# A graph-attention kernel on one core: chunks of blocks of 5, 8, 12 and 12 tiles in place of 8, 11, 11 and 7, rows in one ring, and a plan with more half steps

## The chip, the core and the metric

The kernel runs on one core of one Trainium2 chip. The metric is the device time in microseconds (us) of one execution. Before the change the median of three runs is 6028.87 us (6024.4 to 6030.63).

The engines are TensorE (PE in the profile; PEld is its weight load), VectorE (DVE), ScalarE (ACT), GpSimd (POOL) and the queue of SyncE (SP), which here only issues transfers. Each works through its own instructions in the order in which the program lists them.

## The reference

A layer of graph attention over 12,500 nodes and 412,500 edges (each of 200,000 in both directions, and a loop at every node), sorted by `dst`. Features are 128 wide, edge features 64.

```python
h = relu(layernorm(x))
h0, q, k, v = h @ Wn + bn, h @ Wq + bq, h @ Wk + bk, h @ Wv + bv
eh = edge_attr_64 @ We + be
attn_in = concatenate([q[src], k[dst], eh], axis=-1)
hmid = leaky_relu(attn_in @ A1 + b1, 0.2)
scores = leaky_relu(hmid @ A2 + b2, 0.2)
w = softmax(scores.mean(axis=-1), axis=0)            # over all edges
out = segment_sum(w[:, None] * v[dst], src, num_segments=12500)
y = h0 + out
x + gamma * (y - mean(y)) / sqrt(var(y) + 1e-5) + beta
```

## The kernel before, in words

**Edges come sorted by `dst` and are needed by `src`.** So the kernel sorts them on the way, in two stages that meet in tables in HBM. A *group* is 1024 edges (8 tiles of 128); there are 403 groups. A *block* is the 128 source nodes whose number leaves the same rest by 98; there are 98 blocks. A table has, for every block, room for a fixed number of tiles of 128 *slots*; a slot takes one edge's row of 257 numbers: its place in the block, the 128 of its hidden vector (without the q part) and the 128 of v.

The groups are cut into four *chunks* by `CHUNKS` (L55, L127 to L136), each with a table of its own. Before the change they hold 86, 121, 121 and 75 groups, and their blocks have 8, 11, 11 and 7 tiles.

- **Getting a chunk ready** (`ready`, L532): counts how many edges each block gets, and gives every edge its slot (`place_slots`, L455). This goes on by *slot steps* of 5 tiles of edges: two matmuls on PE into one bank (L478), a reduction on DVE (L522), a comparison on DVE (L471), a small scaling (L526). 646 of them in all: 138, 194, 194 and 120 for the four chunks. `clear_ends` (L163) writes zeros over the last two tiles of every block of a table.
- **First stage** (`first_stage`, L655): for each group, loads edge features, a window of k and v, and the offsets; in four *half steps* it makes rows with PE (L705, L708), moves them out of PSUM with ACT (L691), and lets POOL scatter each tile of 128 rows into its slots by an indirect DMA (L645, eight for a group).
- **Second stage** (`second_stage`, L718): for each block of a chunk, loads its slots (`load`, L725), adds the q part by a selection of nodes, takes the leaky ReLU, the scores, the exponentials against a running maximum, and sums the weighted v rows by node into `acc`. It works on *quads* of up to 4 tiles: two quads for blocks of 7 and 8 tiles, three for 11 and 12.

**What runs beside what.** L1012 to L1027 make five stretches. In the first, chunk 0 goes through its first stage while chunk 1 is made ready. In the next ones the second stage of a chunk runs beside the first stage of the chunk after it and beside the making ready of the one after that. In the last one only the second stage of chunk 3 is left. `interleave` (L63) puts the steps of these jobs in turn, by their shares. Before all this come the nodes' own matmuls, and after it a final normalisation.

**The plan of the second stage** (L871 to L905). A block i begins at step `2 * i0`; a quad takes two steps, so that blocks of two quads come every 4 steps and blocks of three every 6. `at(when, turn_, job, ...)` puts a job into a step and into one of four places in it (turn 0 to 3); jobs of the same place go by the number of the block, older first. Several blocks are under way at a time, each at another link of this chain: `turn` (PE: transposes and adds q), `steep` (ACT scales by 0.2, then DVE takes the larger of the two), `heads_of` (PE), `add_bias` (ACT), `leaky` (DVE), `by_slot` (PE), `scores` (DVE), `turn_top` (PE), `top_of_all` (DVE), `spread_top` (PE), `exponentials` (DVE, then ACT), `add_weights` and `weights` (DVE), `products` (PE), `add_sums` (DVE). All of it is in this order on the engines' queues: an engine that waits for one job holds back all that is listed behind it. Before it come `load`, then `places` (PE turns the places of the rows), `put_places` (ACT, and a DMA to HBM), `spread_places` (a DMA that spreads them over all partitions) and `select` (DVE).

Rows are held in a pool of six buffers of 11 tiles (`BUFS`, L37). A load is planned 17 steps ahead of its block (11 for two quads), and not before the `products` of the block six earlier (`load_at`, L907); `places` is planned 7 steps ahead. `LAG` (L35) is the number of steps from a block's start to its first `products`.

Of the kernel before, what the change touches and what calls it, by code (L numbers as in the profile page):

```python
# [10 lines left out]
FP = mybir.dt.float32  # L11
BF = mybir.dt.bfloat16
# [3 lines left out]
AF = mybir.ActivationFunctionType  # L16
ALU = mybir.AluOpType
AX = mybir.AxisListType
# [4 lines left out]
P = 128  # L23
D = 128
DE = 64
H = 8
EPS = 1e-5
SLOPE = 0.2
# [3 lines left out]
WIN = 42  # L32

QUAD = 4
LAG = 11  # L35

BUFS = 6  # L37

RROWS = 16

SPARE = 2

OTHER = 960

STR = 5

# [2 lines left out]
ROW = 2 * D + 1  # L49
# [2 lines left out]
MAGIC = float(3 << 22)  # L52

NGRP = 5
CHUNKS = (0.213, 0.3, 0.3, 0.187)  # L55
BECAUSE = "worked out within these bounds on the chip"


def _ceil(a, b):
    return -(-a // b)  # L60
# [44 lines left out]
def kernel(ctx: ExitStack, tc: tile.TileContext, n_edges, x, src, dst, ea, w_nv, w_qt, w_kt,  # L105
# [12 lines left out]
    nc = tc.nc  # L118
    NP = x.shape[0]
    NTN = NP // P  # L120
# [14 lines left out]
    NC = len(chunks)  # L135
    most_tiles = max(ct for _, _, ct, _ in chunks)  # L136

    blocks = []
    for c, (_, _, ct, _) in enumerate(chunks):
        for b in range(NTN):  # L140
            blocks.append((c, b, ct, _ceil(ct, QUAD), blocks[-1][4] + blocks[-1][3] if blocks else 0))
        assert 2 * QUAD >= ct > QUAD or 3 * QUAD >= ct > 2 * QUAD
# [6 lines left out]
    q_tab = dram.tile([NTN, P, 3 * D], BF, name="q_tab")  # L149
# [23 lines left out]
    ident = const.tile([P, P], FP, name="ident")  # L173
# [5 lines left out]
    ones = const.tile([P, P], FP, name="ones")  # L179
# [59 lines left out]
    t_bank = ps_t.tile([P, 512], FP, name="t_bank")  # L239
# [215 lines left out]
    def place_slots(c):  # L455
# [31 lines left out]
        def settle(t0, t1):  # L487
# [116 lines left out]
    most_of = late.tile([P, NTN], FP, name="most_of")  # L604
# [20 lines left out]

    main = ctx.enter_context(ExitStack())
    p1 = main.enter_context(tc.tile_pool(name="p1", bufs=2))
    pb = main.enter_context(tc.tile_pool(name="pb", bufs=BUFS))
# [4 lines left out]
    p3 = main.enter_context(tc.tile_pool(name="p3", bufs=1))  # L633
# [5 lines left out]
    def scatter(c, g, k, row, sent):  # L639
# [3 lines left out]
        if m > 0:  # L643
# [74 lines left out]
    def second_stage():  # L718


        rows_of, qws, plss, state = {}, {}, {}, {}
        state["s_ps"] = ps_s.tile([P, 512], FP, name="s_ps")
        nc.vector.memset(state["s_ps"], 0.0)

        def load(i):  # L725
            c, b, ct, _, _ = blocks[i]
            rows_of[i] = pb.tile([P, most_tiles, ROW], FP, name="rows_of")
            nc.sync.dma_start(out=rows_of[i][:, 0:ct, :],
                              in_=tabs[c][b * ct * P:(b + 1) * ct * P, :].rearrange("(p j) r -> p j r", p=P))
            qws[i] = ps.tile([P, 3 * D], BF, name="qw")  # L730
            nc.sync.dma_start(out=qws[i], in_=q_tab[b])

        def places(i):
            ct = blocks[i][2]
# [8 lines left out]

        def spread_places(i):
            ct = blocks[i][2]
            plss[i] = p1.tile([P, most_tiles * P], U8, name="pls")
            at = i % 4 * most_tiles
            nc.sync.dma_start(out=plss[i][:, 0:ct * P], in_=pl_d[at:at + ct, :].rearrange("t e -> (t e)").unsqueeze(0)
                              .to_broadcast([P, ct * P]))
# [8 lines left out]
        def turn(i, q):  # L758
# [7 lines left out]
            for k in range(3):  # L766
                nc.tensor.matmul(h_ps[:, 0:m * P], lhsT=qws[i][:, ts(k, D)], rhs=plss[i][:, q * QUAD * P:(q * QUAD + m) * P],  # L767
                                 start=False, stop=k == 2, skip_group_check=True)

        def steep(i, q):  # L770

            m = min(QUAD, blocks[i][2] - q * QUAD)
            h_ps = state.pop((i, q))[:, 0:m * P]
            low = p3.tile([P, QUAD * P], FP, name="low")[:, 0:m * P]
            nc.scalar.activation(low, h_ps, AF.Copy, scale=SLOPE)  # L775
# [39 lines left out]
            nc.vector.tensor_reduce(state["top"], score[:, 0:ct], AX.X, ALU.max)  # L815

        def turn_top(i):
            nc.tensor.transpose(state["s_ps"][0:1, P:2 * P], state["top"], ident)

        def top_of_all(i):  # L820
            state["top1"] = ps.tile([1, 1], FP, name="top1_of")
            nc.vector.tensor_reduce(state["top1"], state["s_ps"][0:1, P:2 * P], AX.X, ALU.max)

        def spread_top(i):
            nc.tensor.matmul(state["s_ps"][:, 2 * P:2 * P + 1], lhsT=ones[0:1, :], rhs=state["top1"], start=True, stop=True,
                             skip_group_check=True)

        def exponentials(i):
            _, b, ct, _, _ = blocks[i]
            before = (b - 1) % NTN  # L830
            nc.vector.tensor_max(most_of[:, b:b + 1], state["s_ps"][:, 2 * P:2 * P + 1], most_of[:, before:before + 1])

            shift = ps.tile([P, 1], FP, name="shift_of")
            nc.vector.tensor_scalar(shift, most_of[:, b:b + 1], -1.0 / H, None, op0=ALU.mult)
            score = state["score", i][:, 0:ct + 1]
            nc.scalar.activation(score, score, AF.Exp, bias=shift, scale=1.0 / H)

        def add_weights(i):
            _, b, ct, _, _ = blocks[i]
# [33 lines left out]
        def at(when, turn_, job, *args):  # L873
            plan_of.setdefault(when, []).append((turn_, len(plan_of[when]) if when in plan_of else 0, job, args))

        for i, (c, b, ct, nq, i0) in enumerate(blocks):
            t = 2 * i0
            at(load_at(i), 2, load, i)
            at(t - 7, 3, places, i)
            at(t - 6, 0, put_places, i)  # L880
            at(t - 5, 0, spread_places, i)
            at(t - 1, 3, select, i)
            for q in range(nq):
                at(t + 2 * q, 1, turn, i, q)
                at(t + 2 * q + 1, 0, steep, i, q)
            t += 2 * nq
            at(t - 1, 3, heads_of, i)
            at(t, 0, add_bias, i)
            at(t, 3, leaky, i)
            at(t + 1, 0, by_slot, i)  # L890
            at(t + 1, 3, scores, i)
            at(t + 2, 0, turn_top, i)
            at(t + 2, 3, top_of_all, i)
            at(t + 3, 0, spread_top, i)
            at(t + 3, 2, exponentials, i)
            at(t + 4, 3, add_weights, i)
# [10 lines left out]
    def load_at(i):  # L907

        _, _, _, nq, i0 = blocks[i]
        t = 2 * i0 - (17 if nq > 2 else 11)  # L910
        if i >= BUFS:
            _, _, _, nq, i0 = blocks[i - BUFS]
            t = max(t, 2 * (i0 + nq - 1) + LAG)
        return t

    def all_sums():

# [8 lines left out]
    def other_edges():  # L926

        with tc.tile_pool(name="others", bufs=1) as op, tc.tile_pool(name="others_ps", bufs=1, space=PSUM) as ops_:
# [5 lines left out]
            with tc.For_i(0, turns, 1) as g:  # L934
# [63 lines left out]
                with tc.For_i(0, NTN, 1) as b:  # L998
# [8 lines left out]
                    nc.vector.tensor_add(a, a, bank[:, 0:D])  # L1007

    second = second_stage()
    ends = [load_at(c * NTN) for c in range(NC)]  # L1010
    ends.append(2 * (blocks[-1][4] + blocks[-1][3]) + LAG)
    for c in range(NC + 1):  # L1012
        jobs = []
        if c < NC:
# [79 lines left out]
```

## Time and profile before

The profile is of one execution of its own: its span is 6619.4 us and its time 6621.16 us, against the median of 6028.87 us of the runs that are not profiled. Lengths in the text come from this execution.

| engine | busy us | share of the span |
|---|---|---|
| PE | 5232.6 | 79% |
| DVE | 4482.4 | 68% |
| POOL | 3374.8 | 51% |
| PEld | 3539.8 | 53% |
| ACT | 2122.2 | 32% |

Busy shares are means over stages that are limited by different things, so the stretches are looked at one by one. Their borders are seen in the first and last instructions of the lines that belong to one job: POOL's first scatter begins at 369.0 us and its last at 5702.8 us, the second stage's loads begin at 1393.7 us, and the last `add_sums` stands at 6476.0 us. A row of a table of stretches gives, for each engine, its busy time and the number of its instructions there, then the granted share of TensorE's clock (1.00 is full speed), the busy share of the 16 DMA engines, and GB/s.

### The profile page before, as it was taken

The numbers are of one execution on the slowest core, as the hardware profiler recorded it, in microseconds if no ns is written. First come the engines' busy times: TensorE is split into PE (matmuls) and PEld (weight loads), VectorE is DVE, ScalarE is ACT, GpSimd is POOL, SyncE is SP. The second block draws the span as 40 slices with busy tenths as digits, with TensorE's granted clock in tenths as the row PEclk, the third lists the DMA queues.
The fourth block names the chain that finished last, engine by engine and source line by source line (L and its number), as shares of the span: only waits on it lengthen the run. The fifth ranks groups of instructions, "written<-read, shape, count | busy, mean of one in ns | idle before, by whom it ended". The sixth has DMA issues, their size and how long they took to land. (4 is left out here: it accounts for less than half of the span.)

```text
span 6619.4 us, 99836 instructions
## 1 busy us (share of the span) xinstructions
PE 5232.6 (79%) x32180; PEld 3539.8 (53%) x32180; DVE 4482.4 (68%) x14096; ACT 2122.2 (32%) x5090; POOL 3374.8 (51%) x3236
## 2 busy tenths in 40 slices
PE   5665665568888888879888888888999999988881
PEld 3332433345555555556555555555766767655550
DVE  8755755556666666657666666665777777777778
ACT  3422122223333333333333333333433333333331
POOL 0057567765666666656666666665555555200000
PEclk8777677778898888989999999989999999999995
DMA  6755455566777777767778777776887878544443
GB/s 192 218 169 158 135 159 155 155 180 202 220 226 215 224 213 221 223 207 231 234 238 248 241 236 226 226 234 212 262 257 250 260 246 260 190 152 152 152 139 117
DMA packets 607563, 1362.14 MB, mean 206 GB/s; under 512 B 120100, under 2 KB 336860, under 8 KB 569016
## 3 DMA queue, kind: packets, MB, share of 16 engines
q1 hardware_dynamic: 423572, 880.87, 46.3%
q0 software_dynamic: 154704, 424.26, 17.7%
q10 hardware_dynamic: 28756, 50.57, 2.4%
q8 instruction: 255, 4.18, 0.3%
q14 instruction: 276, 2.26, 0.1%
HBM read 782.14 MB, written 573.14 MB: 205 GB/s over the span
## 5 line engine op out<-in xcount | busy, mean ns | idle before, releaser
L645 POOL DMA_INDIRECT tab<-row,slots x3223 | 3373.1, 1047 | 2328.3 <-ACT row L691 861.8
L691 ACT ACTIVATE row<-row_ps 128x512 f32<-128x512 f32 x1612 | 948.4, 590 | 1438.4 <-PE row_ps L708 611.1
L705 PE MATMUL row_ps<-w_ea,ea_t 128*128 128x256 f32 x3224 | 1106.4, 428 | 101.0 <-ACT row L691 55.0
L859 PE MATMUL o_ps<-rows_of,w 128*128 128x128 f32 x7252 | 1122.7, 298 | 59.2 <-DVE w L850 31.6
L776 DVE TENSOR_TENSOR rows_of<-h_ps,low 128x512 f32<-128x512 f32 (+1 forms) x980 | 634.9, 648 | 648.4 <-ACT low L775 446.5
L850 DVE TENSOR_SCALAR w<-iota_f,rows_of,score 128x128 f32<-128x128 f32 x3626 | 1022.3, 350 | 10.4
L859 PEld LDWEIGHTS o_ps<-rows_of,w 128*128 128x128 f32 x7252 | 945.0, 200 | 104.2 <-DVE w L850 56.1
L775 ACT ACTIVATE low<-h_ps 128x512 f32<-128x512 f32 (+1 forms) x980 | 551.6, 563 | 1176.8 <-PE h_ps L767 544.5
L705 PEld LDWEIGHTS row_ps<-w_ea,ea_t 128*128 128x128 f32 x3224 | 624.9, 213 | 462.0 <-issue 220.8
L767 PE MATMUL h_ps<-sel_q,qw 128*128 128x512 bf16 (+1 forms) x2940 | 778.7, 375 | 8.3 <-DVE sel_q L755 8.1
L522 DVE TENSOR_REDUCE num<-run 128x5 f32<-128x500 f32 x646 | 433.2, 671 | 404.2 <-remote 200.0
L708 PE MATMUL row_ps<-kv,sel 126*128 126x256 bf16 x3224 | 679.5, 295 | 11.7 <-DVE sel L681 11.1
L784 PE MATMUL s_ps<-rows_of,a_sb 128*32 128x512 f32 (+1 forms) x1960 | 515.2, 616 | 121.5 <-issue 48.2
L764 PE MATMUL h_ps<-ident,rows_of 128*128 128x128 f32 x3626 | 591.4, 284 | 0.3 <-issue 0.3
L478 PE MATMUL run<-one,rest_b 128*128 128x500 f16 x642 | 276.9, 431 | 341.5 <-DVE num L522 259.6
L801 PEld LDWEIGHTS s_ps<-heads,z 96*128 96x128 f32 (+1 forms) x3136 | 394.9, 195 | 216.7 <-DVE z L795 151.4
L764 PEld LDWEIGHTS h_ps<-ident,rows_of 128*128 128x128 f32 x3626 | 450.4, 147 | 110.7 <-issue 86.1
L708 PEld LDWEIGHTS <-sel 126*128 126x128 bf16 x3224 | 343.7, 107 | 301.4 <-issue 70.4
L801 PE MATMUL s_ps<-heads,z 96*128 96x3 f32 (+1 forms) x3136 | 415.1, 253 | 106.1 <-DVE z L795 83.8
L791 ACT ACTIVATE z<-s_ps,b_col 64x512 f32<-64x512 f32 (+1 forms) x392 | 267.2, 682 | 647.7 <-PE s_ps L784 410.5
L471 DVE TENSOR_TENSOR one<-bins_b,block 128x500 f16<-128x500 bf16 x646 | 431.0, 667 | 0.3 <-PE run L478 0.3
L795 DVE SCALAR_TENSOR_TENSOR z<-z 64x512 f32<-64x512 f32 (+1 forms) x392 | 267.2, 682 | 207.7 <-ACT z L791 165.7
(178 smaller groups left out, 4791.4 us busy)
## 6 DMA issues: line engine op xcount, KB each, us to landing
rows_of<-tab SPq DMA_DIRECT2D x196, 1413.5 KB
ea_t<-in_ea SPq DMA_DIRECT2D x403, 256.0 KB
tab<-blank SPq DMA_DIRECT2D x392, 257.0 KB
rows_of<-tab SPq DMA_DIRECT2D x98, 1028.0 KB
rows_of<-tab SPq DMA_DIRECT2D x98, 899.5 KB
tab<-row,slots POOLq DMA_INDIRECT x3223
offs<-off_d SPq DMA_DIRECT2D x403, 126.0 KB
qw<-q_tab SPq DMA_DIRECT2D x392, 96.0 KB
```

Source lines behind the costliest of these rows:

```text
L645: i = nc.gpsimd.indirect_dma_start(out=tabs[c][:, :], out_offset=bass.IndirectOffsetOnAxis(ap=slots[c][t // (8 * STR)][:m, t % (8 * STR):t ...
L691: nc.scalar.activation(row[:, :, 1:ROW], bank, AF.Copy)
L705: nc.tensor.matmul(bank[:, :, 0:D], lhsT=ea_g[:, ts(k, P)], rhs=w_ea, start=True, stop=False, skip_group_check=True)
L708: nc.tensor.matmul(bank[:, b, :], lhsT=sel[:, ts(b * halves + k, P)], rhs=kv, start=False, stop=True, skip_group_check=True)
L764: nc.tensor.matmul(h_ps[:, ts(j, P)], lhsT=rows_of[i][:, q * QUAD + j, 1:D + 1], rhs=ident, is_transpose=True, start=j == 0, stop=False, s ...
L767: nc.tensor.matmul(h_ps[:, 0:m * P], lhsT=qws[i][:, ts(k, D)], rhs=plss[i][:, q * QUAD * P:(q * QUAD + m) * P], start=False, stop=k == 2, ...
L775: nc.scalar.activation(low, h_ps, AF.Copy, scale=SLOPE)
L776: nc.vector.tensor_max(rows_of[i][:, q * QUAD:q * QUAD + m, 1:D + 1], h_ps.rearrange("p (j e) -> p j e", j=m), low.rearrange("p (j e) -> p ...
L784: nc.tensor.matmul(state["s_ps"][32 * q:32 * (q + 1), 0:m * P], lhsT=a2_sb, rhs=rows_of[i][:, q * QUAD:q * QUAD + m, 1:D + 1], start=True, ...
L801: nc.tensor.matmul(state["s_ps"][:, 0:nq * QUAD].rearrange("p (q j) -> p j q", j=QUAD)[:, j, :], lhsT=state["z"][:32 * nq, ts(j, P)], rhs= ...
L850: nc.vector.tensor_scalar(w, iota_f, rows_of[i][:, t, 0:1], state["score", i][:, t:t + 1], op0=ALU.is_equal, op1=ALU.mult)
L859: nc.tensor.matmul(state["o_ps"][:, 0:D], lhsT=w, rhs=rows_of[i][:, t, D + 1:ROW], start=t == 0, stop=t == ct - 1)
```

## The change

- `CHUNKS` makes chunks of 52, 86, 132 and 133 groups, whose blocks have 5, 8, 12 and 12 tiles. Tiles of slots are 3626 in all, as before, and quads 980, as before; two quads a block in the first two chunks, three in the last two. Slot steps become 84, 138, 212 and 213.
- Rows are held in one ring of 65 tiles (`RING`): a block takes as many tiles as it has. A load is planned 16 steps ahead of its block (`LEAD`), not before the one ahead of it, and not before the last `products` of the blocks whose tiles it takes. With blocks of 12 tiles the ring holds five, and the plan puts the load 11 steps ahead of its block; with 5 and 8 tiles it is 16.
- `places` comes 10 steps ahead, or 4 after the load if that is later (7 ahead with 12 tiles); `spread_places` also loads the block's q, which `load` did.
- The links of the chain stand further apart, most by half a step; `flat` (ACT's part of `steep`) and `greatest` (DVE's part of `exponentials`) are jobs of their own; `LAG` is 13 for two quads and 15 for three, where it was 11.
- `turn_top` and `spread_top` write into `t_bank`, not into the bank `s_ps` that `heads_of` writes.
- `OTHER` (the length of the area for edges without a slot) is 840, where it was 960.

```diff
-LAG = 11
-BUFS = 6
+LAG = {2: 13, 3: 15}
+RING = 65
+LEAD = 16
-CHUNKS = (0.213, 0.3, 0.3, 0.187)
+CHUNKS = (0.1295, 0.2145, 0.328, 0.328)
...
+            here = ring_at[-1] + blocks[-1][2] if i else 0
+            here = here if here + ct <= RING else 0
+            when = max(2 * i0 - LEAD, load_at[-1] if i else -LEAD)
+            for k in range(max(0, i - 2 * RING // QUAD), i):
+                _, _, ct0, nq0, k0 = blocks[k]
+                if ring_at[k] < here + ct and here < ring_at[k] + ct0:
+                    when = max(when, 2 * (k0 + nq0 - 1) + LAG[nq0])
+            ring_at.append(here)
+            load_at.append(when)
+            blocks.append((c, b, ct, nq, max(i0, (when + 9) // 2)))
...
+            rows_of[i] = ring[:, ring_at[i]:ring_at[i] + ct, :]
+            nc.sync.dma_start(out=rows_of[i], in_=tabs[c][b * ct * P:(b + 1) * ct * P, :].rearrange("(p j) r -> p j r", p=P))
...
         def spread_places(i):
             ct = blocks[i][2]
+            qws[i] = ps.tile([P, 3 * D], BF, name="qw")
+            nc.sync.dma_start(out=qws[i], in_=q_tab[blocks[i][1]])
...
+        def flat(i, q):
+            m = min(QUAD, blocks[i][2] - q * QUAD)
+            state["low"] = p3.tile([P, QUAD * P], FP, name="low")[:, 0:m * P]
+            nc.scalar.activation(state["low"], state[i, q][:, 0:m * P], AF.Copy, scale=SLOPE)
...
-            nc.tensor.transpose(state["s_ps"][0:1, P:2 * P], state["top"], ident)
+            nc.tensor.transpose(t_bank[0:1, P:2 * P], state["top"], ident)
...
-            at(load_at(i), 2, load, i)
-            at(t - 7, 3, places, i)
-            at(t - 6, 0, put_places, i)
-            at(t - 5, 0, spread_places, i)
+            at(load_at[i], 2, load, i)
+            u = max(t - 10, load_at[i] + 4)
+            at(u, 3, places, i)
+            at(u + 1, 2, put_places, i)
+            at(u + 2, 2, spread_places, i)
             at(t - 1, 3, select, i)
             for q in range(nq):
                 at(t + 2 * q, 1, turn, i, q)
-                at(t + 2 * q + 1, 0, steep, i, q)
+                at(t + 2 * q + 1, 2, flat, i, q)
+                at(t + 2 * q + 2, 0, steep, i, q)
             t += 2 * nq
-            at(t - 1, 3, heads_of, i)
-            at(t, 0, add_bias, i)
-            at(t, 3, leaky, i)
-            at(t + 1, 0, by_slot, i)
-            at(t + 1, 3, scores, i)
-            at(t + 2, 0, turn_top, i)
-            at(t + 2, 3, top_of_all, i)
-            at(t + 3, 0, spread_top, i)
-            at(t + 3, 2, exponentials, i)
-            at(t + 4, 3, add_weights, i)
-            t = 2 * i0 + LAG
+            at(t, 3, heads_of, i)
+            at(t + 1, 2, add_bias, i)
+            at(t + 2, 0, leaky, i)
+            at(t + 2, 3, by_slot, i)
+            at(t + 3, 2, scores, i)
+            at(t + 4, 2, turn_top, i)
+            at(t + 5, 0, top_of_all, i)
+            at(t + 5, 3, spread_top, i)
+            at(t + 6, 2, greatest, i)
+            at(t + 7, 0, exponentials, i)
+            at(t + 8, 0, add_weights, i)
+            t = 2 * i0 + LAG[nq]
             for q in range(nq):
                 at(t + 2 * q - 1, 0, weights, i, q)
                 at(t + 2 * q, 1, products, i, q)
```

`weights`, `products` and `add_sums` stand as before against the new `LAG`.

More of the change, by code (lines that the diff above doesn't have):

```diff
@@ L34 @@
 QUAD = 4
-LAG = 11
-BUFS = 6
+LAG = {2: 13, 3: 15}
+RING = 65
+LEAD = 16
 RROWS = 16
 SPARE = 2
-OTHER = 960
+OTHER = 840
 STR = 5
@@ L136 @@
     most_tiles = max(ct for _, _, ct, _ in chunks)
-    blocks = []
+    blocks, ring_at, load_at = [], [], []
     for c, (_, _, ct, _) in enumerate(chunks):
+        nq = _ceil(ct, QUAD)
+        assert nq in LAG
         for b in range(NTN):
-            blocks.append((c, b, ct, _ceil(ct, QUAD), blocks[-1][4] + blocks[-1][3] if blocks else 0))
-        assert 2 * QUAD >= ct > QUAD or 3 * QUAD >= ct > 2 * QUAD
+            i0 = 0
+            if blocks:
+                _, _, _, nq0, i0 = blocks[-1]
+                i0 += nq0 + max(0, LAG[nq0] - LAG[nq]) // 2
+            i = len(blocks)
+            here = ring_at[-1] + blocks[-1][2] if i else 0
[8 more added lines that the diff above has]
+            blocks.append((c, b, ct, nq, max(i0, (when + 9) // 2)))
     const = ctx.enter_context(tc.tile_pool(name="const", bufs=1))
@@ L627 @@
     p1 = main.enter_context(tc.tile_pool(name="p1", bufs=2))
-    pb = main.enter_context(tc.tile_pool(name="pb", bufs=BUFS))
+    pb = main.enter_context(tc.tile_pool(name="pb", bufs=1))
     ps = main.enter_context(tc.tile_pool(name="ps", bufs=5))
@@ L723, in second_stage @@
         nc.vector.memset(state["s_ps"], 0.0)
+        ring = pb.tile([P, RING, ROW], FP, name="rows_of")
         def load(i):
             c, b, ct, _, _ = blocks[i]
[L727 to L731, printed above, removed]
+            rows_of[i] = ring[:, ring_at[i]:ring_at[i] + ct, :]
+            nc.sync.dma_start(out=rows_of[i], in_=tabs[c][b * ct * P:(b + 1) * ct * P, :].rearrange("(p j) r -> p j r", p=P))
         def places(i):
@@ L773, in steep @@
             h_ps = state.pop((i, q))[:, 0:m * P]
-            low = p3.tile([P, QUAD * P], FP, name="low")[:, 0:m * P]
-            nc.scalar.activation(low, h_ps, AF.Copy, scale=SLOPE)
+            low = state["low"]
             nc.vector.tensor_max(rows_of[i][:, q * QUAD:q * QUAD + m, 1:D + 1],
@@ L817, in turn_top, with greatest @@
         def turn_top(i):
-            nc.tensor.transpose(state["s_ps"][0:1, P:2 * P], state["top"], ident)
+            nc.tensor.transpose(t_bank[0:1, P:2 * P], state["top"], ident)
         def top_of_all(i):
             state["top1"] = ps.tile([1, 1], FP, name="top1_of")
-            nc.vector.tensor_reduce(state["top1"], state["s_ps"][0:1, P:2 * P], AX.X, ALU.max)
+            nc.vector.tensor_reduce(state["top1"], t_bank[0:1, P:2 * P], AX.X, ALU.max)
         def spread_top(i):
-            nc.tensor.matmul(state["s_ps"][:, 2 * P:2 * P + 1], lhsT=ones[0:1, :], rhs=state["top1"], start=True, stop=True,
+            nc.tensor.matmul(t_bank[:, 2 * P:2 * P + 1], lhsT=ones[0:1, :], rhs=state["top1"], start=True, stop=True,
                              skip_group_check=True)
-        def exponentials(i):
[L829 to L836, printed above, removed]
+        def greatest(i):
+            b = blocks[i][1]
+            before = (b - 1) % NTN
+            nc.vector.tensor_max(most_of[:, b:b + 1], t_bank[:, 2 * P:2 * P + 1], most_of[:, before:before + 1])
+            state["shift"] = ps.tile([P, 1], FP, name="shift_of")
+            nc.vector.tensor_scalar(state["shift"], most_of[:, b:b + 1], -1.0 / H, None, op0=ALU.mult)
+        def exponentials(i):
+            score = state["score", i][:, 0:blocks[i][2] + 1]
+            nc.scalar.activation(score, score, AF.Exp, bias=state["shift"], scale=1.0 / H)
         def add_weights(i):
@@ L905, in second_stage @@
             yield
[L907 to L914, printed above, removed]
     def all_sums():
@@ L1009 @@
     second = second_stage()
-    ends = [load_at(c * NTN) for c in range(NC)]
-    ends.append(2 * (blocks[-1][4] + blocks[-1][3]) + LAG)
+    ends = [load_at[c * NTN] for c in range(NC)]
+    ends.append(2 * (blocks[-1][4] + blocks[-1][3]) + LAG[blocks[-1][3]])
     for c in range(NC + 1):
```

## The prediction, made before the changed kernel was run

> **What bounds the kernel now.** I read the table of stretches first, cut where POOL's scatters and the second stage begin and end; then the waits of each stretch, then the order in time inside two of them. Call the rows A (nodes), B (chunk 0's first stage alone), C, D, E (both stages) and F (chunk 3's second stage alone), G (the end).
>
> ```profile
> core 0: us, PE busy (x) PEld busy (x) DVE busy (x) ACT busy (x) POOL busy (x), PEclk, DMA share, GB/s
> 0.00:369.00 369.00, 229.00 (x1457) 124.11 (x1458) 273.48 (x875) 146.22 (x475) 1.70 (x13) 0.84 0.72 205
> 369.00:1399.00 1030.00, 620.24 (x3014) 342.57 (x3012) 600.61 (x1661) 221.88 (x518) 714.10 (x689) 0.72 0.50 152
> 1399.00:2958.00 1559.00, 1271.56 (x7602) 867.35 (x7603) 1006.19 (x3245) 507.70 (x1203) 1001.56 (x969) 0.87 0.73 217
> 2958.00:4593.00 1635.00, 1369.43 (x8640) 964.96 (x8639) 1058.45 (x3326) 557.00 (x1313) 1023.22 (x969) 0.92 0.74 232
> 4593.00:5703.00 1110.00, 1062.31 (x7113) 776.03 (x7114) 818.76 (x2640) 435.05 (x1040) 633.45 (x599) 1.00 0.79 253
> 5703.00:6482.00 779.00, 679.46 (x4357) 464.30 (x4355) 595.71 (x2134) 234.42 (x501) 0.79 (x1) 0.98 0.46 144
> 6482.00:6619.00 137.00, 0.59 (x2) 0.50 (x2) 129.17 (x222) 19.96 (x41) 0.00 (x0) 0.50 0.44 141
> ```
>
> PE is busy 96% of E and over 80% of C and D, but 60% of B. F, with nothing beside it, is a chain of short waits. POOL's busy time hides its limit: two scatters never start closer than 0.96 us and an idle 0.30 behind it, 1.26 us, so B's 688 need 867 of 1030 us, C's and D's 968 need 1220 each, E's 600 need 756.
>
> ```profile
> 2060.39 0.96 POOL L645 DMA_INDIRECT tab<-row,slots  x1 [0.30 <-issue]
> ```
>
> In B, C and D there are also moments when all of PE, DVE and ACT stand for 1 to 9 us, ended by nothing that the profile knows ("remote" in the waits). I add up 160, 112 and 103 us of them; E and F have none. Runs without a profile are 590 us shorter, so I hold most of these, and the lower clock behind them, for the profile's own.
>
> **What a block costs.** F's waits and its order in time:
>
> ```profile
> PEld s_ps L825 <- DVE top_of L822: 99.0, 98, 1.9
> PEld s_ps L801 <- DVE z L795: 77.9, 99, 2.4
> PEld t_bank L735 <- DMA rows_of<-tab: 2.8, 1, 2.8
> ```
> ```profile
> 6005.99 1.05 PE L784 MATMUL s_ps<-rows_of,a_sb 128*32 128x512 f32 x4
> 6006.97 0.66 PE L764 MATMUL h_ps<-ident,rows_of 128*128 128x128 f32 x4
> 6007.46 0.81 PE L767 MATMUL h_ps<-sel_q,qw 128*128 128x512 bf16 x3
> 6008.55 1.05 PE L801 MATMUL s_ps<-heads,z 64*128 64x2 f32 x8 [0.28 <-DVE z L795]
> 6010.77 1.11 DVE L850 TENSOR_SCALAR w<-iota_f,rows_of,score 128x128 f32<-128x128 f32 x4
> ```
>
> A block of 7 tiles comes every 7.52 us (starts 6005.99 and 6013.51). PE waits 0.45 of it for z and 0.79 for the top: 6.28 us are work. One tile more is 0.12 (transpose) + 0.16 (q) + 0.11 (heads) + 0.24 (products) = 0.63: 5.0 us for 5 tiles, 6.9 for 8, 8.8 for 11, 9.4 for 12. A half step of the first stage is about 0.7 (L705 at 2058.36 to the next at 2059.11); a slot step 0.85 (two L478 in 0.42, five L408 at 85 ns). **Test on before**, at the granted clock and with the standing moments: C (98x6.9 + 484x0.7 + 194x0.85)/0.87 + 112 = 1468 of 1559 (94%); D 1519 of 1635 (93%); E 98x8.8 + 300x0.7 = 1072 of 1110 (97%). PE bounds C, D and E.
>
> **The change, stretch by stretch.** The work is the same in sum (403 groups, 3626 tiles, 980 quads, 646 slot steps give or take one), so what counts is where it lies.
>
> *B* goes from 86 groups to 52, its slot steps from 313 to some 206. By scatters 416 x 1.497 (1030/688) = 623; by slot steps 206 x 3.29 (1030/313) = 678; floor 524. I take **650** (-380).
>
> *C*: 86 groups with blocks of 5 and 212 slot steps: 490 + 241 + 180 = 911; at clock 0.86, +115 standing, at 93.5%: 1256. `turn_top` and `spread_top` leave the bank s_ps, so C's waits of heads for `most_of` (47.2 us) go; what is late next is PE itself, so I credit 20: **1235**. DVE's work falls to some 880, POOL's floor is 867.
>
> *D*: 132 groups, blocks of 8, 213 slot steps: 676 + 370 + 181 = 1227; at 0.88, +115, at 93.5%: 1614, less 20: **1595**. POOL's floor is 1056 x 1.26 = 1331, hidden here, though not in a run without standing moments (1227/0.93 = 1320).
>
> *E*: 133 groups, blocks of 12, no slot steps: 926 + 372 = 1298, /0.966 = 1344. POOL's floor is 1064 x 1.26 = 1341. Two engines at their limit do not mesh: before, E's mean spacing was 1.86. Between 1345 and 1480 I take **1410** (5% above the floor).
>
> *F*: 98 blocks of 12, alone, and here the new order must be walked. Modulo 6 DVE's list is: step 0 w of the third quad, steep 2, greatest; step 2 `add_sums`, `add_weights`, w of the first, leaky, steep 0; step 3 scores; step 4 w of the second, steep 1; step 5 top, select. PE's: turn 0, heads; products 2; turn 1, by_slot; products 0; turn 2, turn_top; products 1, spread_top, places. With F's rows (four w 1.11, steep 0.69, leaky 0.68, sums and weights 0.35 + 0.41, select 0.68 x 12/7 less a fixed part = 1.06): w to 1.11, steep 2 to 1.80. Heads waits for it, 1.87 to 3.37 (1.28 and the gap that F's heads show); products 2 to 4.4, result 4.55. **`add_sums` waits for just that and heads DVE's list**, behind it leaky: 4.60 + 0.35 + 0.41 + 1.11 + 0.68 gives leaky at 7.15. by_slot, 1.7 us late on PE, 7.2 to 8.2; steep 0 and the scores to 8.65; w and steep 1 to 10.45; turn_top ends 10.57, top to 10.89, select to 11.95, where the next w begins. Each period of **11.95 us** has 9.2 of DVE's work and 2.45 of waiting for products 2; PE works 9.4. So the half steps move the wait, they do not end it: 98 x 11.95 + 26 steps of filling and draining at 2.0 = **1220** (+441). Clock stays at 0.98: no PE gap exceeds 1.7 us.
>
> *A* and *G* stay at 369 and 137. `flat` and `greatest` are the same instructions moved; ACT is busy 30% in F. `spread_places` moves q's load behind the places on SP, off the load's instruction and ahead of the next load by 0.42 us.
>
> **The ring.** With 12 tiles a load waits for the last products of the block five earlier, and `places` follows 4 steps later, where 11-tile blocks had 10. Behind `places` stand all of PE, and behind the load on SP the first stage's three loads. In F: from 4.6 to 11.7 planned, and turn 0 can begin as late as 12.6 before it delays heads: room 7.9 us. F's load of 0.9 MB has landed after 4.62 us (median over the trace's semaphore records), its data taking 3.3 of these; 12 tiles give 4.62 + 5/7 x 3.3 = 7.0, and places and q, just ahead, add up to 1. It just fits; nothing is added. The Trainium skill ("DMA: Bandwidth & Descriptors", section "Anatomy of one DMA") fits 2.0 us and bytes at 436 GB/s: 1.58 MB in 5.6 us, 2.3 us to spare. The fit is of loads from GpSimd's queue; I go by the row, which leaves no margin. In E, 11 tiles took 8.3 us to their last packet beside scatters; 12 give 9.3 with the landing, against some 9.0 between products 2 and `places` at a period of 14: up to 0.5 us a block, 50 us, inside E's 1410.
>
> **Sum.** 369 + 650 + 1235 + 1595 + 1410 + 1220 + 137 = 6616 against 6619 (the execution took 6621): no change in the profiled execution. In the timed runs B's gain is smaller: without its 160 us of standing, 34/86 of 870 is 344, 36 less. 6029 x 6616/6619 + 36 = 6062.
>
> **Rivals.**
> 1. *Faster: the half steps do end the waits.* DVE's place in step 2 is then not decisive: F runs at PE's 9.4 us and 8% (10.2, 1050 us in all), C and D at 96% (1210, 1560), E at POOL's 1370. Sum 6346; timed, 6346/6619 x 6029 + 36 = 5816; half of it 5940. For it: E already runs at 97% of PE. Against it: the walk, in which `add_sums` stands before leaky. It decides if F's period is below 11.0 us.
> 2. *Slower: the loads of 12 tiles come late.* If they land 1.5 us beyond the room, every one of 196 blocks of E and F waits on PE: 196 x 1.5 = 294, timed about 6350; a third of that, 6160. For it: lead of 4 steps, E's DMA share of 0.79 before. Against: F's single wait of 2.8 us. It decides from a landing of 8 us in F, 9.5 in E.
> 3. *The ring does nothing that shows, the chunks all:* B and F cancel (-344 and +441) with C to E gaining 100: within 0.2% of 6029.
>
> **Chances.** The forecast, 6062, with its own range 5990 to 6130: 0.5, of which 0.31 slower by over 0.2% (about what a measurement of this kernel can tell from no change), 0.08 within (rival 3), 0.11 faster. Rival 1: 0.29, all faster. Rival 2: 0.21, all slower. Together faster 0.40, same 0.08, slower 0.52. The range leaves out the outer half of either rival: 5880 to 6230.
>
> **What would show it.** Per stretch: B near 650, F near 1220 with starts of `add_sums` 11.95 apart; DVE waiting for products before `add_sums` some 2.4 us a block; by_slot waiting for z; no `most_of` wait of heads; POOL spaced 1.26 to 1.35 in E. A wait of `places` for rows_of above 20 us in F or 60 in E speaks for rival 2; an F below 1080 for rival 1. The forecast is wrong if C and D together differ from 2830 by over 120, too.

## The result and the profile after

The changed kernel takes 6282.03 us (median of 4 runs, 6267.81 to 6297.7), the kernel before beside it on the same chip 6029.75 (4 runs, 6024.4 to 6042.76): a ratio of 1.0416, with a 95% interval of 1.0385 to 1.0446. It is slower by 252 us. The forecast was 6062 us, its widest range 5880 to 6230.

Chips differ: the kernel before takes 6030 to 6073 us on some (called the faster chips below) and 6608 to 6714 on others (the slower ones). The profile ahead of the prediction, with 6621 us, belongs with the slower, and the comparison above was made on a faster one. So times are compared on one chip, as ratios, or in F, which is nearly alike on both kinds (773 to 779 us before). To have both tables of stretches from one chip, both kernels were profiled again one after the other (before_third and after_third below: 6082.65 and 6300.99 us). These are the rows B to F of before; the columns are those of the table ahead of the prediction.

```profile
372.00:1317.00 945.00, 618.00 (x3092) 347.63 (x3091) 604.56 (x1685) 214.69 (x523) 718.49 (x689) 0.78 0.53 166
1317.00:2633.00 1316.00, 1167.76 (x7412) 810.40 (x7514) 989.81 (x3212) 501.61 (x1197) 1008.46 (x967) 0.93 0.85 254
2633.00:4064.00 1431.00, 1282.65 (x8511) 936.34 (x8618) 1052.06 (x3321) 561.96 (x1309) 1026.27 (x968) 0.95 0.85 265
4064.00:5171.00 1107.00, 1051.37 (x7063) 778.42 (x7162) 821.00 (x2659) 444.37 (x1047) 643.74 (x599) 0.99 0.80 256
5171.00:5944.00 773.00, 670.40 (x4286) 460.02 (x4336) 594.38 (x2127) 233.54 (x499) 0.00 (x0) 0.99 0.46 145
```

The same rows of the changed kernel:

```profile
344.00:918.00 574.00, 374.74 (x1923) 208.15 (x1922) 389.00 (x1093) 129.54 (x311) 433.93 (x416) 0.78 0.61 181
918.00:1981.00 1063.00, 938.81 (x6254) 644.02 (x6349) 866.04 (x3029) 388.54 (x992) 719.15 (x691) 0.93 0.81 227
1981.00:3417.00 1436.00, 1255.74 (x7987) 859.67 (x8089) 1062.88 (x3447) 518.16 (x1286) 1094.04 (x1054) 0.95 0.80 245
3417.00:4927.00 1510.00, 1281.22 (x8176) 920.13 (x8323) 896.57 (x2801) 595.21 (x1388) 1157.07 (x1063) 0.96 0.80 256
4927.00:6162.00 1235.00, 998.55 (x6212) 698.80 (x6311) 812.05 (x2719) 284.31 (x597) 0.00 (x0) 0.91 0.46 150
```

Read the fifth pair, POOL, with 0.30 us of issue added for each scatter. Here are three scatters in a row in the changed kernel's E, from its order in time:

```profile
4200.75 0.96 POOL L664 DMA_INDIRECT tab<-row,slots  x1 [0.30 <-issue]
4202.02 1.82 POOL L664 DMA_INDIRECT tab<-row,slots  x1 [0.30 <-issue]
4204.15 0.96 POOL L664 DMA_INDIRECT tab<-row,slots  x1 [0.30 <-issue]
```

Most take 0.96 us, but 16% of them take more than 1.2 us and the longest 2.5: the mean in this E is 1157.07/1063 = 1.09, a scatter costs 1.39 with its issue, and 1063 of them 1157 + 319 = 1476 of 1510 us. POOL's queue has next to nothing left over. So it is in B and in D of the changed kernel and in B and C of before; what POOL leaves idle (length, less busy time, less 0.30 for each scatter) is

| | A | B | C | D | E | F | G |
|---|---|---|---|---|---|---|---|
| before, us | 372 | 945 | 1316 | 1431 | 1107 | 773 | 137 |
| after, us | 344 | 574 | 1063 | 1436 | 1510 | 1235 | 137 |
| difference | -28 | -371 | -253 | +5 | +403 | +462 | 0 |
| POOL idle before | | 20 | 17 | 114 | 284 | | |
| POOL idle after | | 15 | 137 | 26 | 34 | | |

This is the whole result. All 3223 scatters lie in B to E and are not made fewer: with 0.30 us each they hold POOL some 4370 us in both kernels. The four stretches together lose 216 us, from 4799 to 4583: POOL idles 212 us in them in place of 435. F, in which POOL has nothing to do, grows by 462.

This holds on the faster chips. On a slower one (after_again, 6890.84 us) the changed kernel's E is longer, and POOL's queue does not fill it:

```profile
3841.00:5528.00 1687.00, 1372.49 (x8305) 971.28 (x8306) 883.99 (x2791) 587.53 (x1387) 1143.70 (x1063) 0.92 0.72 229
```

There 1144 + 319 = 1463 of 1687 us are POOL's, and 224 it idles.

F itself, in the first profile of the changed kernel (one of the four timed runs, 6279.02 us; A to F are 341, 573, 1048, 1433, 1510 and 1235). Its waits, and the order in time around one block, lines left out:

```profile
DVE acc L893 <- PE o_ps L884: 274.0, 102, 5.6
PEld s_ps L824 <- DVE z L818: 181.1, 100, 2.6
PEld t_bank L752 <- DMA rows_of<-tab: 101.1, 55, 11.1
```
```profile
5504.67 0.28 PE L752 MATMUL t_bank<-ident,rows_of 128*12 128x128 f32 x1 [0.48 <-DMA rows_of<-tab]
...
5505.79 0.14 DVE L854 TENSOR_TENSOR most_of<-t_bank,most_of 128x1 f32<-128x1 f32 x1
5505.96 0.27 ACT L757 ACTIVATE plT<-t_bank 12x128 uint8<-12x128 f32 x1 [2.44 <-DVE most_of L854]
5506.25 0.31 SPq L759 DMA_DIRECT2D pl_d<-plT  x1
...
5508.16 0.35 DVE L893 SCALAR_TENSOR_TENSOR acc<-acc,score,o_ps 128x128 f32<-128x128 f32 x1 [2.05 <-PE o_ps L884]
...
5509.55 0.32 SPq L767 DMA_DIRECT2D pls<-pl_d  x1
...
5509.98 0.37 SPq L748 DMA_DIRECT2D rows_of<-tab  x1
...
5510.51 1.05 PE L824 MATMUL s_ps<-heads,z 96*128 96x3 f32 x8 [1.31 <-DVE z L818]
...
5518.29 0.38 PE L752 MATMUL t_bank<-ident,rows_of 128*12 128x128 f32 x1 [3.33 <-DMA rows_of<-tab]
```

Three things are to be seen. `add_sums` (5508.16) heads DVE's list and waits 2.05 us for products; behind it `by_slot` (5510.51) waits 1.31 for z, as walked. The places' way out, pl_d at 5506.25, must land before it is read as pls at 5509.55, and SP holds back all that stands behind pls: the next load of rows leaves at 5509.98, although its tiles came free with the products that `add_sums` waited for. This is one of the longer of these waits: in the whole of F, SP waits 69.2 us for pl_d to land (98 times, 2.6 at most), and 82.1 us more, 53 times, for the products that free the tiles. And plT (5505.96) starts right behind `greatest` (5505.79), which reads the same bank.

### The profile page after: what moved, and what is told of

It reads as the page before. It is cut to its first block, busy times and chain, and to the rows that moved or that the text cites. A ratio compares the mean times of both kernels' runs of the same rounds, so it can differ in the third digit from the quotient of the medians.

```text
span 6277.1 us, 99268 instructions
## 1 busy us (share of the span) xinstructions
PE 5089.7 (81%) x32182; PEld 3441.3 (55%) x32182; DVE 4421.0 (70%) x14106; ACT 2079.7 (33%) x5090; POOL 3412.3 (54%) x3236
## 5 line engine op out<-in xcount | busy, mean ns | idle before, releaser
L664 POOL DMA_INDIRECT tab<-row,slots x3223 | 3410.6, 1058 | 1490.0 <-issue 754.0
L884 PE MATMUL o_ps<-rows_of,w 128*128 128x128 f32 x7252 | 1047.6, 288 | 0.9 <-DVE w L875 0.9
L724 PEld LDWEIGHTS row_ps<-w_ea,ea_t 128*128 128x128 f32 x3224 | 554.8, 205 | 614.7 <-ACT row L710 340.0
L786 PE MATMUL h_ps<-sel_q,qw 128*128 128x512 bf16 (+1 forms) x2940 | 799.0, 383 | 23.8 <-DVE sel_q L774 20.4
L792 ACT ACTIVATE low<-h_ps 128x512 f32<-128x512 f32 x980 | 545.0, 556 | 749.6 <-DVE none L832 336.9
L799 DVE TENSOR_TENSOR rows_of<-h_ps,low 128x512 f32<-128x512 f32 x980 | 625.9, 639 | 56.7 <-ACT low L792 56.7
L824 PE MATMUL s_ps<-heads,z 64*128 64x2 f32 (+1 forms) x3136 | 418.2, 254 | 261.0 <-DVE z L818 261.0
L824 PEld LDWEIGHTS s_ps<-heads,z 64*128 64x128 f32 (+1 forms) x3136 | 384.5, 191 | 412.7 <-DVE z L818 375.8
L893 DVE SCALAR_TENSOR_TENSOR acc<-acc,score,o_ps 128x128 f32<-128x128 f32 x294 | 101.6, 345 | 641.0 <-PE o_ps L884 640.7
L707 ACT ACTIVATE row<-place 128x4 f32<-128x4 bf16 x806 | 164.5, 204 | 1172.6 <-DMA tab<-row,slots 1153.9
```

Source lines behind the costliest of these rows:

```text
L664: i = nc.gpsimd.indirect_dma_start(out=tabs[c][:, :], out_offset=bass.IndirectOffsetOnAxis(ap=slots[c][t // (8 * STR)][:m, t % (8 * STR):t ...
L724: nc.tensor.matmul(bank[:, :, 0:D], lhsT=ea_g[:, ts(k, P)], rhs=w_ea, start=True, stop=False, skip_group_check=True)
L792: nc.scalar.activation(state["low"], state[i, q][:, 0:m * P], AF.Copy, scale=SLOPE)
L824: nc.tensor.matmul(state["s_ps"][:, 0:nq * QUAD].rearrange("p (q j) -> p j q", j=QUAD)[:, j, :], lhsT=state["z"][:32 * nq, ts(j, P)], rhs= ...
L884: nc.tensor.matmul(state["o_ps"][:, 0:D], lhsT=w, rhs=rows_of[i][:, t, D + 1:ROW], start=t == 0, stop=t == ct - 1)
```

## The experiments

Stretches of every run in us, and the ratio to the kernel before with its interval, where one was taken. Each set ran on a chip of its own: those of sets 1 and 2 are slower ones, those of 3 and 4 faster. The times in us that the expectations of set 1 name are for a chip on which the kernel before takes 6030 us; on that of set 1 it takes 6714, so what counts is the stretches and the ratios.

| set | run | A | B | C | D | E | F | ratio |
|---|---|---|---|---|---|---|---|---|
| 1 | before_again | 372 | 1039 | 1577 | 1660 | 1145 | 775 | |
| 1 | load_first | 343 | 636 | 1214 | 1713 | 1727 | 1249 | 1.0391 (1.0362 to 1.042) |
| 1 | sums_late | 343 | 638 | 1189 | 1695 | 1694 | 1116 | 1.0189 (1.0161 to 1.0216) |
| 1 | old_chunks | 371 | 1039 | 1572 | 1618 | 1282 | 758 | 1.0148 (1.0121 to 1.0176) |
| 2 | after_again | 341 | 629 | 1193 | 1678 | 1687 | 1229 | 1.0425 (1.0395 to 1.0456) |
| 2 | new_chunks_old_plan | 344 | 632 | 1655 | 2203 | 1700 | 1011 | 1.1624 (1.1591 to 1.1658) |
| 2 | old_chunks_ring66 | 369 | 1027 | 1556 | 1590 | 1189 | 759 | 1.0028 (1.0015 to 1.004) |
| 2 | old_chunks_ring66_sums_late | 365 | 1029 | 1539 | 1565 | 1097 | 726 | 0.9786 (0.9754 to 0.9818) |
| 3 | before_third | 372 | 945 | 1316 | 1431 | 1107 | 773 | |
| 3 | after_third | 344 | 574 | 1063 | 1436 | 1510 | 1235 | |
| 3 | thin_q | 343 | 576 | 1064 | 1434 | 1484 | 1222 | 1.0336 (1.0311 to 1.0361) |
| 3 | sums_late_load_first | 342 | 577 | 1026 | 1440 | 1677 | 1320 | 1.0703 (1.0679 to 1.0728) |
| 4 | after_fourth | 345 | 577 | 1070 | 1440 | 1511 | 1212 | |
| 4 | extra_scatter | 343 | 572 | 1062 | 1433 | 1665 | 1212 | 1.0607 (1.059 to 1.0625) |
| 4 | best_again | 371 | 941 | 1319 | 1392 | 1084 | 726 | 0.9841 (0.9823 to 0.9858) |

**The two kernels again.** before_again and before_third, after_again, after_third and after_fourth give the stretches of each set.

> The kernel before, unchanged, to have a profile of an execution as fast as its timed runs. Expected: near 6030 us, no moments of 1 to 9 us in which PE, DVE and ACT all stand. If POOL's queue sets the stretches with a first stage, stretch B (first stage of chunk 0 alone) takes 860 to 900 us, near 688 scatters at 1.26 us, F (last chunk's second stage alone) 779 as before, and C, D and E together 3850 to 3950. If the standing moments belong to the kernel, the profile shows them again and 6600 us.

> The changed kernel, unchanged, beside the next three on one chip. Expected: the ratio of 1.042 of the first comparison, within 0.01, whatever the chip's own speed; F 1220 to 1250 us on every chip, since nothing scatters in it.

> The kernel before as it is, with a profile on the chip of this set. F 776 whatever the chip. If this chip runs it in some 6030 us, its profile has few standing moments, and POOL's busy time with 0.30 us for each scatter fills B, C and D to 95% or more (theory POOL); if it runs it in some 6700, POOL fills them to 80%.

> The changed kernel as it is, for its stretches on the chip of this set: ratio 1.042; E and F as long as in proportion before (E 1.09 to 1.11 of what D is by POOL's queue on a fast chip, F 1229 to 1236).

> The changed kernel as it is, for its stretches on the chip of this set: ratio 1.04; E 1510 us with POOL's scatters 0.3 us behind one another on a fast chip, 1690 us with gaps on a slow one.

A profiled execution takes no longer than one without: 6705.46 against a median of 6714.2 us in set 1, 6082.65 against 6071.08 in set 3. So before_again missed its 6030 us. In the kernel before, the moments over 1 us in which PE, DVE and ACT all stand add up to some 424 us on the chip of set 1 and 175 on that of set 3, most of it in B, C and D on both: the profile does not bring them, and how many there are goes with the chip. In the changed kernel they reach E as well: 105 us of it in after_again, 39 in after_third, where before_again has 10 and before_third none. F is the same on both (775 and 773), and the ratio of the changed kernel differs little between a chip where before takes 6030 us and one where it takes 6608 (1.0416 and 1.0425).

**Is F held by the load that stands behind the places on SP?**

```diff
-            at(u + 2, 2, spread_places, i)
+            at(u + 2, 3, spread_places, i)
```

> The changed kernel with spread_places moved from turn 2 to turn 3 of its step, so that the next load of rows stands ahead of it on SP's queue and no longer waits until the places have landed in HBM. Theory 1 (POOL's queue fills B, D and E, and F is added to it): E stays within 20 us of 1508, F loses its waits for rows (about 100 us), time 6150 to 6190. Theory 2 (late loads of 12 tiles set E and F): E and F each lose 80 us or more, time below 6120. If the loads are late for their length and not for their place in the queue: unchanged, 6270 to 6290.

F's waits after it:

```profile
DVE acc L893 <- PE o_ps L884: 201.7, 100, 3.0
...
DVE sel_q L774 <- DMA pls<-pl_d: 87.1, 70, 4.9
```

PE's waits for rows are gone but for 4 us, and F is no shorter: 1249 us (1229 in set 2). The places now stand behind 1.5 MB of rows, and `select` waits for them. One wait was traded for another, so this run alone does not clear the load; the next one does.

**Is F held by `add_sums` at the head of DVE's list?**

```diff
-            at(t + 2 * nq - 1, 0, add_sums, i)
+            at(t + 2 * nq - 1, 3, add_sums, i)
```

> The changed kernel with add_sums moved from turn 0 to turn 3 of its step, so that on DVE the weights, leaky and steep no longer stand behind a wait for the products of an older block. Theory 3 (that order sets F's undisturbed period of 10.8 us): the period goes to 9.7 or less, F loses 80 to 110 us, time 6160 to 6200; DVE's wait for products (274 us in F) falls below 100. Theory 1: E does not change, whatever F does. If F is set by the loop from products over load and places back to products: F unchanged within 20 us.

F goes from 1229 us (set 2) to 1116; the median time between starts of `add_sums` goes from 11.83 to 10.42 us, less far than the 9.7 expected. DVE's wait for products is down to 0.5 us; what heads PE's waits is

```profile
PEld t_bank L752 <- DMA rows_of<-tab: 196.2, 97, 4.3
```

PE waits for rows twice as long as before (101 us), and F is 113 us shorter: the wait of `add_sums` held F, and the loads stood behind it. What comes next is a ring: a load and its landing (6.8 us from issue to `places`, median), 0.5 to plT, 0.3 to pl_d, and 2.7 to the next load on SP make 10.3 us. In the last part SP waits for pl_d to land (63.3 us in F) and, longer, for the products that free the tiles (115.2 us, 82 times), 0.03 us behind which the load leaves in the median; those stand on PE behind the same `places`.

**Both edits together.**

> The changed kernel with both of the edits that were tried alone: add_sums at the end of its step, and places behind the next load on SP. Theory: with add_sums off the head of DVE's list, F is held by the wait for rows (190 us at PE with add_sums alone moved), so that both together give F at PE's 9.4 us a block and some 970 us, E 60 less than with add_sums alone; ratio 1.00. Rival: select then waits for the places, as it did with the load moved alone (87 us in F), and F stays at 1110 or more; ratio 1.02.

Both expectations were missed: 1.0703, slower than with either edit alone, E 1677 and F 1320 us. POOL idles 273 us in this E, so here its queue does not set it. The order in time in F:

```profile
5602.42 0.38 PE L752 MATMUL t_bank<-ident,rows_of 128*12 128x128 f32 x1 [2.24 <-DMA rows_of<-tab]
...
5605.66 0.15 DVE L854 TENSOR_TENSOR most_of<-t_bank,most_of 128x1 f32<-128x1 f32 x1
5605.84 0.27 ACT L757 ACTIVATE plT<-t_bank 12x128 uint8<-12x128 f32 x1 [6.33 <-DVE most_of L854]
...
5606.13 0.32 SPq L759 DMA_DIRECT2D pl_d<-plT  x1
...
5609.57 0.34 SPq L748 DMA_DIRECT2D rows_of<-tab  x1
...
5616.46 0.28 PE L752 MATMUL t_bank<-ident,rows_of 128*12 128x128 f32 x1 [1.66 <-DMA rows_of<-tab]
```

The places are turned at 5602.42, but plT leaves at 5605.84, behind `greatest` on the bank that the change moved it to; `greatest` stands on DVE behind `select`, which waits for the pls that were issued behind the rows (303.3 us in F, 98 times). Then the next load waits on SP for products:

```profile
SPq L748 <- PE o_ps L884: 213.5, 97, 3.2
```

and the weights for these stand on DVE behind `greatest` too. So the ring closes through all of them: 6.5 to `places`, 3.5 to plT, 0.3 to pl_d and 2.7 to the next load make 13.0 us (medians), and a load leaves every 13.2. Two edits that each cut one wait are not worth their sum where both waits lie in one ring.

**Which part does it, the chunks or the plan?** old_chunks is the changed kernel with the old chunks; new_chunks_old_plan is the kernel before with the new ones, for which its pool of rows must shrink.

```diff
-CHUNKS = (0.1295, 0.2145, 0.328, 0.328)
+CHUNKS = (0.213, 0.3, 0.3, 0.187)
```
```diff
-BUFS = 6
-OTHER = 960
-CHUNKS = (0.213, 0.3, 0.3, 0.187)
+BUFS = 5
+OTHER = 840
+CHUNKS = (0.1295, 0.2145, 0.328, 0.328)
```

> The changed kernel with the chunks of before (86, 121, 121, 75 groups; 8, 11, 11 and 7 tiles): ring and wider links alone. Theory 1: the loss is the chunks': F returns to 780 to 850 us, B to 860 to 900, time at or below before, 5900 to 6040. Theory 2 (ring and links lose): blocks of 11 tiles, of which the ring also holds five, wait for their loads in D and E too, and the time stays above 6100.

> The kernel before with the chunks of the change (52, 86, 132, 133 groups; 5, 8, 12 and 12 tiles), its own plan of links, LAG 11, and buffers for five blocks (six of 12 tiles do not fit): the chunks alone. Theory 1 (the chunks lose: F grows and POOL has nothing to gain): F is 1080 to 1200 us, the ratio 1.02 to 1.05, near that of the whole change. Theory 2 and 3 (the new plan loses, by late loads or by add_sums before leaky): the ratio is below 1.01 and E runs 100 us or more shorter than in the whole change.

F of 12-tile blocks takes 1011 us under the old plan, less than the 1080 expected, and 1229 under the new one. At 9.88 us a block it lies near the 9.4 that the prediction gave PE's own work. So of F's growth some 236 us (1011 - 775) are the larger blocks and some 218 the new plan, which was made to end waits. With two quads a block the new plan costs F nothing (758). E is the same under both plans (1700, 1687, on the slower chip). The ratio, 1.1624, was not expected by either theory and says nothing of the chunks: it comes from C and D, where five buffers put the load of a two-quad block into the step of its `places`, and PE waits 1276.5 us for rows (191 of 196 blocks).

old_chunks met neither theory: F came back, but its E is 137 us longer than before's. Its waits there:

```profile
DVE acc L893 <- PE o_ps L884: 239.0, 79, 5.0
...
PEld t_bank L752 <- DMA rows_of<-tab: 79.8, 50, 3.9
```

**Is that E held by the ring?** 65 tiles hold five blocks of 11; 66 hold six.

```diff
-RING = 65
+RING = 66
```

> The chunks of before in the plan of the change, with a ring of 66 tiles where it has 65: six blocks of 11 tiles fit, and the plan puts their loads 16 steps ahead of the block and places 6 steps after the load, where it was 11 and 4. Theory 2 (late loads): stretch E, 1282 us with a ring of 65 against 1144 before, comes back to 1150 or less, its waits of PE for rows go, and the ratio to before falls from 1.015 to below 1.0. Theory 3 (the order on DVE): E stays above 1230.

> The same with add_sums in turn 3 of its step. Theory 3: E falls by 60 us or more against the run before this one and its period of a block goes to 11.5 us or less; F's to 7.2 or less; with D 60 us shorter than before the ratio is 0.975 to 0.99. Theory 2: no more than 20 us between the two.

With one tile more, PE's waits for rows are gone from E. E is 1189 us after 1282 (on two of the slower chips; 1150 was expected), and the ratio, each against before on its own chip, goes from 1.0148 to 1.0028: rows that come late do cost, where POOL has room (here its 600 scatters fill two thirds of E). With `add_sums` moved too, E falls to 1097, F to 726, and the ratio to 0.9786: faster than both kernels.

**What fills E of the changed kernel, PE, POOL or the waits?** First less of PE's work, then more of POOL's.

```diff
-            for k in range(3):
+            for k in range(1):
...
-                                 start=False, stop=k == 2, skip_group_check=True)
+                                 start=False, stop=True, skip_group_check=True)
```

> The changed kernel with the first of the three selection matmuls that add the q part, in place of all three: the two low parts of q are left out of the result. It takes two matmuls of 128x512 bf16 (some 0.27 us each at full clock) from PE in every quad, 1.6 us from a block of 12 tiles, 1.0 of 8, 0.7 of 5, and nothing from DVE, POOL or the loads. Theory PE (PE's own work sets the stretches where both stages run): E loses 98 x 1.6 / 0.96 = 160 us, D 100, C 70; ratio to the kernel before near 0.99. Theory POOL (the queue of scatters fills B, D and E, and DVE's walk sets F): C to E together lose under 60 us, F under 30; ratio 1.03 to 1.045. Theory chain (waits for late loads and for add_sums set E): E and F lose under 40 each, as with POOL.

Its rows E and F:

```profile
3417.00:4901.00 1484.00, 1200.22 (x7634) 904.40 (x7733) 896.95 (x2801) 602.63 (x1388) 1132.29 (x1063) 0.91 0.81 260
4901.00:6123.00 1222.00, 917.73 (x5618) 688.34 (x5717) 807.40 (x2719) 284.32 (x597) 0.00 (x0) 0.87 0.46 151
```

C to E lose 27 us against after_third, F 13. PE is busy 81 us less in E, where 160 were expected; its clock is lower too (0.91 for 0.96). E is 26 us shorter, and POOL's own busy time there is 25 less: PE's work holds none of these stretches.

```diff
+            if c == NC - 1 and k == 0:
+                i = nc.gpsimd.indirect_dma_start(
+                    out=spare[:, :], out_offset=bass.IndirectOffsetOnAxis(ap=slots[c][t // (8 * STR)][:m, t % (8 * STR):t % (8 * STR) + 1], axis=0),
+                    in_=row[:m, :], in_offset=None)
```

> The changed kernel with one more scatter for every group of chunk 3, of a row tile that has just been scattered, into a table of its own that nothing reads: 133 more of POOL's indirect DMAs, all in E, and nothing more on PE, DVE or ACT. Theory POOL: its queue fills E, so E grows by 133 x 1.39 = 185 us and the ratio to the kernel before by 0.03, to 1.07. Theory chain (late loads and the wait of add_sums set E, POOL fills up around them): E grows by under 60 us. D, which has none of them, stays.

E without it (after_fourth) and with it:

```profile
3431.00:4942.00 1511.00, 1285.90 (x8176) 919.38 (x8323) 896.88 (x2801) 591.71 (x1388) 1160.06 (x1063) 0.96 0.79 255
```
```profile
3410.00:5076.00 1666.00, 1351.66 (x8176) 964.06 (x8323) 899.20 (x2801) 583.99 (x1388) 1280.31 (x1196) 0.92 0.75 242
```

133 scatters more make E 155 us longer, nearly what POOL's queue asks: its busy time grows by 120 and its issue by 133 x 0.30 = 40. The 185 expected were too many because the mean scatter fell from 1.09 to 1.07 us. D is as before. POOL's queue sets E, on the faster chips on which these two runs were made; on the slower ones neither was tried.

**The best version again.**

> The chunks of before (8, 11, 11, 7) with the changed kernel's plan, a ring of 66 tiles and add_sums at the end of its step, measured again beside the kernel before: 0.9786 on the chip where it ran first. If it gains in E and F (E 1145 to 1097, F 775 to 726 there), it gains about 100 us on any chip: 0.98 to 0.985. If POOL's queue fills E here too, E gains nothing and the ratio is 0.99.

```profile
4023.00:5106.00 1083.00, 1030.64 (x7016) 769.67 (x7117) 807.02 (x2639) 448.64 (x1038) 635.77 (x599) 0.98 0.83 262
5106.00:5832.00 726.00, 713.72 (x4344) 469.39 (x4393) 573.94 (x2154) 213.11 (x504) 0.00 (x0) 0.99 0.55 154
```

5974.75 us, 0.9841 (0.9823 to 0.9858). The 98 us are what was expected. Against before_third, on another chip of the same pace, D loses 39, E 23 and F 47: with the old chunks PE is busy 95% of E and 98% of F, POOL idles 267 us in E, and a better order of links is worth something there.

## Why the prediction was wrong

The forecast was made from a profile on a slower chip, and its difference between the two kernels was -3 us. Between the two profiles of one faster chip it is +218; the timed runs were made on such a chip. The last row sets the changed kernel's lengths on a slower chip (after_again) against the lengths that were forecast.

| | A | B | C | D | E | F |
|---|---|---|---|---|---|---|
| forecast, after less before | 0 | -380 | -324 | -40 | +300 | +441 |
| measured, after less before, faster chip | -28 | -371 | -253 | +5 | +403 | +462 |
| measured less forecast length, slower chip | -28 | -21 | -42 | +83 | +277 | +9 |

Of the 221 us that the forecast is short on the faster chip, E has 103, C 71 and D 45.

- **The step that failed: "two scatters never start closer than 0.96 us and an idle 0.30 behind it, 1.26 us".** That is the least of a scatter, and it was used as its price. The rows shown with the prediction had the mean: 633.45/599 = 1.06 in E, 1023.22/968 = 1.06 in D. At 1.36, E's floor is 1064 x 1.36 = 1447 us, not 1341, and so lies above the 1410 that were taken; D's is 1056 x 1.36 = 1436, not 1331. With that, "two engines at their limit do not mesh" and "1410 (5% above the floor)" fall too: on the faster chip a scatter costs 1.39 us in E, E lies 2% above the 1476 us of that queue, and PE has room. thin_q and extra_scatter show that it was POOL in E.
- **On a slower chip this is only a part of it.** There E took 1687 us, 277 more than forecast; POOL's queue at its mean accounts for 53 of them, and in 224 us POOL idles. The prediction put nothing into E for standing moments ("E and F have none"), since the kernel before has hardly any there; the changed kernel has 105 us of them. What holds the rest of this E, and D's 83 us, stays open.
- **C and D, "PE bounds C, D and E".** On the faster chips right only for E of before. POOL fills 99% of before's C and 92% of its D there. So C's gain was 71 us smaller than PE's sum said, since its old length was POOL's, and D could not shrink: its 1056 scatters fill 98% of it afterwards. This is read from how full the queue is; no run put more or fewer scatters into C or D alone.
- **"I hold most of these, and the lower clock behind them, for the profile's own": wrong.** Profiled executions are not slower. The model was fitted to one kind of chip and the timed runs come from another, where the standing moments that covered POOL's queue are fewer. One of its own signs shows it: C and D together were to lie within 120 us of 2830; they took 2871 on a slower chip and 2499 on a faster one. The prediction had the right remark ("hidden here, though not in a run without standing moments") and did not follow it.
- **B: right** (-371), and in the timed estimate of -344 near. On the faster chip POOL's queue fills 97% of it, so the slot steps, by which the higher of its two sums went, did not set it. **A: missed by 28.** "A and G stay" left out that chunk 0's edges are counted in A: 416 small matmuls in place of 688, and 17 steps on DVE in place of 28. DVE is busy 10 us less there and PE 18; the rest was not traced. The slot steps in A are 19 in both.
- **F: right in mechanism and size.** Median period 11.83 us for 11.95, F 1235 for 1220; DVE waits 2.8 us a block for products where 2.45 was walked, by_slot 1.3 to 1.8 for 1.7. sums_late took away that wait and 113 us. But PE stood longer than the 1.7 us allowed there, 21 times and up to 3.7 us, and its clock was 0.91 in F, where before it was 0.99; the forecast had 0.98.
- **The ring, "It just fits; nothing is added": nearly, but for a wrong reason.** "Places and q, just ahead, add up to 1" was too little: from pl_d's issue to the load's it was 1.8 us at least, 2.4 in the median and 4.5 or more in one block of ten, because SP waits for pl_d to land and for products. The landing went as the row said: where PE waited for rows in every block (sums_late and sums_late_load_first) it was 6.5 to 6.8 us from issue to `places`, for 7.0 by the row; the estimate of 5.6 us from the Trainium skill's fit ("DMA: Bandwidth & Descriptors", section "Anatomy of one DMA") was too short for these loads from SP. In the changed kernel PE waits 101 us for rows in F, 55 times; sums_late, where these waits double and F gets shorter, shows that they stood behind DVE's wait.
- **Rivals.** Rival 1 fell: F's period is not below 11. Rival 2's signs came (waits of `places` for rows of 101 us in F and 105 in E; in E 9.6 us in the median from a load's issue to `places` where PE waited), and its mechanism is real, worth 1.2% with the old chunks; but in the changed kernel E is POOL's on the faster chips and F is held by DVE's wait first, so it was not the cause. That its time (6160 to 6350) held the result is luck. Rival 3 fell with E: C to E together did not gain 100 us but grew by 155.

What stays open: why the slower chips stand for more moments where scatters run; what holds the changed kernel's C, in which POOL idles 137 us on a faster chip; and how much F would gain if `greatest` and the places did not share a bank, which was not tried alone.

## What to carry to other kernels

Before work is shifted between stages, find the engine whose total cannot shrink, here POOL with 3223 scatters, and count what it leaves idle in each stage in which it works: a shift can win back no more than that from these stages, and it pays in full for work moved to where that engine has nothing to do. Price an instruction in a queue by its mean with its issue, from the row of the stage, never by its shortest. A ring that goes through a load, its landing, the places' round trip and the products that free the tiles is timed as a whole: cutting one wait in it can lengthen another. And fit a model to a profile from the chip on which the times are taken.

## What was not expected of the hardware

- The same program took 6029 to 6714 us on different chips. The difference lies where scatters run (before's C: 1316 and 1577 us) and not in A (372 and 372) or F (773 and 775).
- An indirect scatter of 128 rows of 1028 bytes took mostly 0.96 us and 1.04 to 1.09 in the mean of a stretch of the two kernels on a faster chip, with 0.30 us between two where the queue is full (99% of the gaps in the changed kernel's E).
- SP's queue waited up to 2.6 us, 0.7 in the mean, for a transfer of 1.5 KB to HBM to land, because a later one reads what it wrote (69.2 us in the changed kernel's F).
